# A lightning-attention and routed-experts block on one core: base projection behind the transposes, routing inside the rounds, experts' second product inside the attention phase

## The chip, the core and the metric

The kernel runs on one core of a Trainium2 chip. A core has five engines with an instruction queue each, and every queue is worked off in order: TensorE (PE, matrix products and transposes), VectorE (DVE), ScalarE (ACT), GpSimd (POOL) and SyncE (SP), which here issues all DMAs. The metric is the device time of one execution in microseconds, as a median over several; beside it stands a profile of a single execution. All data are fp32. A matrix product of fp32 shows in the records as two passes of PE.

## The reference

With x of 2 x 512 tokens and width 512, and xn = layernorm(x):

```python
x = x + _L0_attn_ref(xn, ...) + _L0_ffn_ref(xn, ...)

# attention: 32 heads of 128, linear attention with decay, blocks of 32
qkv = silu(xn @ qkv_w.T)                 # q, k, v
scores = q k^T * diag_decay ; intra = scores v ; inter = (q * q_decay) kv
attn = intra + inter, normalised over all heads (rms), times norm_w
out = (sigmoid(xn @ gate_w.T) * normed) @ out_w.T

# experts: 8 low-rank experts of rank 16, the two largest logits per token
logits = x_flat @ W_router.T ; combine = weights of the top 2, else 0
h = einsum('nd,erd->ner', x_flat, A) ; hw = h * combine[:, :, None]
expert_out = einsum('ner,eor->no', hw, B) * 2
base_out = x_flat @ W_base.T + b_base
```

The feed-forward half (base_out + expert_out) depends only on xn and meets the attention half in the last addition.

## The kernel before

Tokens are eight tiles of 128 (t = 0 to 7). The kernel has four stages.

**Setup** (lines 204 to 335, pool `sp`). SP loads the eight tiles `x`, the router and A weights `wra`, the base weights `wbase`, `bias`, `wlb` (B), and the first two weight sets `raw`. For each tile, DVE normalises (L242 to L248), PE transposes it into a bank `fr` (L252), ACT copies it to `xnT` (L253), PE makes logits and h at once in bank `ra` (L257, recorded under the helper `mm`, L80), and ACT copies them to `lg` and `hl` (L259, L260). `base(t)` (L227) makes the base product in one of four banks `seeded` (in the profile `sd`); it is called three tiles behind the transposes, and DVE adds it to x (L233). Then come the routing on DVE (L278 to L300: two maxima over the logits, their weights, `hl` multiplied by them), sums of `xnT` (`xsum`, L306 to L309, and `xt`, L316 to L319), the bias additions on POOL (L321), and the experts: transposes of `hl` (L326), a copy to `hT` (L329), the product with `wlb` (L333), an addition on DVE (L334) and a store to `x_kept` in DRAM (L335).

**Rounds** (lines 354 to 470, pools `aw` and `aw2`). v and gate of all heads are made with a two-level Strassen scheme: 56 rounds of 7 inner products. `encode` (L173) makes the weight sums on POOL two rounds ahead (`s`, five buffers, and `e`, three); `inner_product` (L354) is PE's; `after` (L386) takes results out of the banks on ACT and DVE into `sum`, `y`, `w`, `c` and `z` (six buffers), and `result` (L374) applies Silu or Tanh and stores v and gate to DRAM. The first two rounds read only the first batch's xnT. `SLOTS` (L443) gives the order by hand: a round's last two products run in the next round.

**Attention** (lines 473 to 690, pool `work`). Loop over i = 0 to 65, two for each head (L652). In each iteration a new `attend` begins (L543), two older ones go on, and parts of the next heads' q and k projections (`unit`, L491) are put between. v and gate come back from DRAM two iterations ahead (`load_vg`, L533, five buffers each). `attend` ends with the output in a bank `at` (two of them), its square on ACT (`sq`, two buffers, L585), the sum of squares on POOL (L586), the gated product on DVE (L588) and a store (L589).

**Output projection** (from L690). It loads `x_kept` back as a whole (`x_back`, L743) and adds it at the end (`finish`, L709).

What sets the order: the code's order gives each instruction its priority; the framework that builds the program orders every engine's queue beforehand, with a model of the times, and takes a later instruction where nothing earlier is ready. So the first sums of the attention's weights (L126) stand on POOL at 49 us, although `load_unit` is called near the end of the rounds. On the chip that order is fixed. Memory of a closed pool is given to the next one, and a tile there waits for the old tiles' last readers.

Of the kernel before, what the change touches and what calls it, by code (L numbers as in the profile page):

```python
# [59 lines left out]
def attn_moe_kernel(ctx: ExitStack, tc: tile.TileContext, x, qk_w, v_w, gate_w, out_w, norm_w,  # L60
# [15 lines left out]
    def bank(tag):  # L76
        return ps.tile([P, 512], F32, tag=tag, name=f"ps_{tag}", bufs=banks[tag])

    def mm(o, lhsT, rhs, start, stop):
        nc.tensor.matmul(o, lhsT, rhs, start=start, stop=stop)  # L80
# [3 lines left out]
    ident = keep.tile([P, P], F32, tag="ident", name="ident")  # L84
    ones = keep.tile([P, 1], F32, tag="ones", name="ones")
    nw = keep.tile([P, H], F32, tag="nw", name="nw")
    xnT = [wts.tile([P, KC, S], F32, tag=f"xnT{b}", name=f"xnT{b}") for b in range(B)]
# [5 lines left out]
                          for i in range(NG // 2)] for n in ("v", "gate"))  # L93
    x_kept = dram.tile([P, NT, HID], F32, tag="x_kept", name="x_kept")

# [77 lines left out]
    def encode(n, q):  # L173

        def outer(k, a, b, op):
            t = sums2[n, k] = aw.tile([P, 2, 2, 256], F32, tag="s", name="s", bufs=5)
            nc.gpsimd.tensor_tensor(t, a, b, op)
# [24 lines left out]


    xt = [aw.tile([P, 4, S // 2], F32, tag=f"xt{q}", name=f"xt{q}") for q in range(1, 8)]
    with tc.tile_pool(name="setup", bufs=1) as sp:
# [4 lines left out]
        wbase = sp.tile([P, KC, HID], F32, tag="wbase", name="wbase")  # L210
        wlb = sp.tile([P, HID], F32, tag="wlb", name="wlb")
        bias = sp.tile([P, HID], F32, tag="bias", name="bias")
        for t in range(NT):
# [3 lines left out]
        nc.sync.dma_start(wbase, base_w)  # L217
        nc.sync.dma_start(bias, base_b.partition_broadcast(P))
        nc.sync.dma_start(wlb, lora_b)
        load_set(0)  # L220
# [6 lines left out]
        def base(t):  # L227

            b, tt = divmod(t, TB)
            bp = seeded[t % 4]  # L230
            for c in range(KC):
                mm(bp, xnT[b][:, c, tt * P : (tt + 1) * P], wbase[:, c, :], c == 0, c == KC - 1)
            nc.vector.tensor_tensor(x_sb[t], x_sb[t], bp, ALU.add)  # L233


        lg = sp.tile([P, NT, NE], F32, tag="lg", name="lg")
        hl = sp.tile([P, NT, NE, R], F32, tag="hl", name="hl")
        stats = sp.tile([P, NT, 6], F32, tag="stats", name="stats")
        mv = sp.tile([P, NT, 2], F32, tag="mv", name="mv")
        for g, ts in enumerate(((0,), (1, 2), (3, 4, 5), (6, 7))):  # L240
# [4 lines left out]
            for i, t in enumerate(ts):  # L245
# [14 lines left out]
                nc.scalar.copy(hl[:, t].rearrange("p e r -> p (e r)"), ra[:, NE : NE + ER])  # L260
                if t > 2:
                    base(t - 3)
        for t in range(NT - 3, NT):
            base(t)

        prio = sp.tile([P, NT, NE], F32, tag="prio", name="prio")
        for e in range(NE):
            nc.gpsimd.memset(prio[:, :, e : e + 1], float(NE - e))

        def small(name, shape):  # L270
            return sp.tile(shape, F32, tag=name, name=name)

        def wide(v):
            return v.unsqueeze(2).to_broadcast([P, NT, NE])

        def largest(lg_, n):
            m, c, hit = small(f"m{n}", [P, NT]), small(f"c{n}", [P, NT]), small(f"hit{n}", [P, NT, NE])
            nc.vector.tensor_reduce(m, lg_, AX.X, ALU.max)  # L278
            nc.vector.tensor_tensor(hit, lg_, wide(m), ALU.is_equal)
            nc.vector.tensor_tensor(hit, hit, prio, ALU.mult)  # L280
            nc.vector.tensor_reduce(c, hit, AX.X, ALU.max)
            nc.vector.tensor_tensor(hit, hit, wide(c), ALU.is_equal)
            return m, hit

        m1, hit1 = largest(lg, 1)
        lg2 = small("lg2", [P, NT, NE])
        nc.vector.scalar_tensor_tensor(lg2, hit1, LOWEST, lg, ALU.mult, ALU.add)
        m2, hit2 = largest(lg2, 2)

        e2, w1, w2 = (small(n, [P, NT]) for n in ("e2", "w1", "w2"))  # L290
        nc.vector.tensor_tensor(e2, m2, m1, ALU.subtract)
        nc.scalar.activation(e2, e2, AF.Exp)
        nc.vector.tensor_scalar_add(w1, e2, 1.0)
        nc.vector.reciprocal(w1, w1)
        nc.vector.tensor_scalar_mul(w1, w1, SCALING)
        nc.vector.tensor_tensor(w2, w1, e2, ALU.mult)
        nc.vector.tensor_tensor(hit1, hit1, wide(w1), ALU.mult)
        nc.vector.tensor_tensor(hit2, hit2, wide(w2), ALU.mult)
        nc.vector.tensor_tensor(hit1, hit1, hit2, ALU.add)
        nc.vector.tensor_tensor(hl.rearrange("p t e r -> p (t e) r"),  # L300
                                hl.rearrange("p t e r -> p (t e) r"),
                                hit1.rearrange("p t e -> p (t e)").unsqueeze(2).to_broadcast([P, NT * NE, R]),
                                ALU.mult)

# [15 lines left out]
        for t in range(NT):  # L320
            nc.gpsimd.tensor_tensor(x_sb[t], x_sb[t], bias, ALU.add)  # L321

        for q in range(NT // 4):
            tp = bank("fr")
            for i in range(4):
                nc.tensor.transpose(tp[:, i * P : (i + 1) * P],  # L326
                                    hl[:, q * 4 + i].rearrange("p e r -> p (e r)"), ident)
            hT = sp.tile([P, 4 * P], F32, tag="hT", name="hT", bufs=2)
            nc.scalar.copy(hT, tp)  # L329
            for i in range(4):  # L330
                t = q * 4 + i
                lp = seeded[i]
                mm(lp, hT[:, i * P : (i + 1) * P], wlb, True, True)  # L333
                nc.vector.tensor_tensor(x_sb[t], x_sb[t], lp, ALU.add)  # L334
                nc.sync.dma_start(x_kept[:, t, :], x_sb[t])  # L335

# [49 lines left out]
    def after(r, i):  # L386
# [6 lines left out]
        def out_of(ij, v, more=None, c=None):  # L393

            for src, to in adds:
                if isinstance(to, str):
                    o = outer_sums[n, to][:, ij]
                else:
                    o = temp("z", 6)
                if more is not None and (src is None or one):  # L400
# [39 lines left out]
        elif i == 4:  # L440
            out_of(2, st["pd"])

    SLOTS = ((0, 1), (0, 5), (0, 2), (1, 7), (0, 6), (0, 3), (1, 4))  # L443
    for k in range(7 * len(rounds) + 7):
        r0, m = divmod(k, 7)
        if m == 0:
            if r0 + 2 < len(rounds):
                encode(*rounds[r0 + 2])
# [94 lines left out]
    def attend(head, b):  # L543
# [37 lines left out]
        if head == 0:  # L581
            nc.scalar.activation(ssq[b], pa, AF.Square)
        else:
            sq = tmp("sq", 2)
            nc.scalar.activation(sq, pa, AF.Square)  # L585
            nc.gpsimd.tensor_tensor(ssq[b], ssq[b], sq, ALU.add)  # L586
# [15 lines left out]
    for _ in projections(0):  # L602
        pass

    HT, HO = S // 2, HID // 2
# [46 lines left out]
    for i in range(H * B + 2):  # L652
        p, part = divmod(i, 4)
        if part == 0:
# [7 lines left out]
            if p == NP - 1:  # L662
# [4 lines left out]
                for j in range(EARLY):  # L667
                    operands(0, j)
        load_vg(i + 2)
        if i < H * B:  # L670
            running[i] = attend(*divmod(i, B))
# [143 lines left out]
```

## Time and profile before

| | us |
|---|---|
| median of 3 runs | 1240.96 (1240.21 to 1243.94) |
| the profiled execution | 1241.71 |
| its span, first to last instruction | 1239.9 |
| setup, to the first round's steady work | 0 to 76.5 |
| rounds | 76.5 to 433 |
| attention | 433 to about 1051 |
| output projection, to the end | about 1051 to 1239.9 |

The page gives, for each engine, busy time and its share of the span, then the span in 40 slices of 31 us. Groups of instructions are named by line, engine, operation and tiles (written <- read), with count, busy time and mean ns of one, and the idle time of the engine before them with what ended it. Busy time of PE is modelled at the ends of its passes, so the distance from start to start is the better measure of what one pass costs. The granted clock tells which share of full speed PE was allowed in a stretch.

### The profile page before, as it was taken

The page shows a single profiled execution, that of the slowest core. Times are in us where ns is not written, and L with a number is a line of the kernel's source. Part 1 is how long each engine was busy: PE and PEld are TensorE (multiplying, and loading weights), DVE is VectorE, ACT ScalarE, POOL GpSimd, SP SyncE. Part 2 cuts the span into 40 slices and gives each one's busy share as a digit, 9 for nine tenths or more (in the row PEclk, how much of TensorE's full clock was granted, in tenths as well). Part 3 has the DMA queues.
Part 4 walks back from the last instruction along what each step waited for, and adds up shares of the span by engine and source line. Part 5 has one row for each costly group of instructions (what it writes and reads, how often), then busy time and mean ns, then how long its engine had stood idle before and what let it go on. Part 6 is the DMA issues. An engine that isn't in the chain of part 4 may idle for free.

```text
span 1239.9 us, 17100 instructions
## 1 busy us (share of the span) xinstructions
PE 1207.4 (97%) x6328; PEld 914.3 (74%) x6328; DVE 629.1 (51%) x1104; ACT 366.1 (30%) x648; POOL 592.8 (48%) x662
## 2 busy tenths in 40 slices
PE   6789999999999999999999999999999999999998
PEld 4369889899899745666666666666666669888887
DVE  5757666766766624444444434444444444455333
ACT  2124444444444422223222222222232332320000
POOL 3926568758756241434433433433333343655552
PEclk9989999999999999999999999999999999999999
DMA  8012543452442353343443443343334333843221
GB/s 315 0 68 75 173 151 121 153 170 96 161 161 103 123 166 91 119 135 112 145 140 103 125 134 102 117 125 118 116 114 128 120 97 108 309 150 122 93 92 52
DMA packets 102706, 158.17 MB, mean 128 GB/s; under 512 B 8800, under 2 KB 68192, under 8 KB 101344
## 3 DMA queue, kind: packets, MB, share of 16 engines
q1 hardware_dynamic: 102624, 157.09, 38.2%
q8 instruction: 50, 0.82, 0.3%
q14 instruction: 32, 0.26, 0.1%
HBM read 102.53 MB, written 54.53 MB: 127 GB/s over the span
## 4 chain that ended last, share of the span: by engine, by line
PE 93%; DVE 5%; issue 1%; ACT 1%; DMA 0%; SPq 0%; DVEq 0%; ACTq 0%
PE ps_ch L488 31%; PE ps_ch L645 9%; PE ps_at L80 8%; PE ps_sc L80 8%; PE ps_fr L362 7%; PE ps_fr L366 7%; PE sd L362 5%; PE sd L366 5%; PE ps_sc L645 4%; PE ps_at L645 2%; PE sd L80 2%; PE ps_sc L550 2%; DVE z L405 1%; DVE sum L405 1%; PE ps_ra L80 1%
## 5 line engine op out<-in xcount | busy, mean ns | idle before, releaser
L488 PE MATMUL ps_ch<-xsum,ws 128*128 128x512 f32 x384 | 180.0, 593 | 0.0
L562 POOL TENSOR_TENSOR qd<-q,mask 128x384 f32<-128x384 f32 x64 | 64.2, 1003 | 219.9 <-PE ps_at L80 214.8
L488 PE MATMUL ps_ch<-xnT,w 128*128 128x512 f32 x256 | 122.2, 600 | 0.8 <-DVE z L405 0.8
L488 PEld LDWEIGHTS ps_ch<-xsum,ws 128*128 128x128 f32 x384 | 68.5, 191 | 63.2 <-issue 63.2
L80 PEld LDWEIGHTS ps_at<-scores,v 128*128 128x128 f32 x512 | 77.4, 192 | 28.0 <-issue 27.7
L126 POOL TENSOR_TENSOR ws<-w 128x256 f32<-128x256 f32 x32 | 23.4, 730 | 154.3 <-DMA w<-in_qk_w 154.3
L503 DVE TENSOR_TENSOR c<-ps_ch,u 128x512 f32<-128x512 f32 x96 | 66.4, 691 | 58.4 <-PE ps_ch L488 58.4
L588 DVE SCALAR_TENSOR_TENSOR gT<-gate,ps_at 128x512 f32<-128x512 f32 x64 | 44.0, 687 | 97.5 <-ACT sq L585 94.5
L645 PE MATMUL ps_ch<-wsum,gsum 128*128 128x256 f32 x384 | 89.1, 379 | 0.0
L80 PE MATMUL ps_at<-scores,v 128*128 128x128 f32 x512 | 88.4, 275 | 0.0
L585 ACT ACTIVATE sq<-ps_at 128x512 f32<-128x512 f32 x62 | 37.0, 597 | 155.2 <-PE ps_at L80 155.1
L586 POOL TENSOR_TENSOR ssq<-ssq,sq 128x512 f32<-128x512 f32 x62 | 79.2, 1278 | 6.5 <-ACT sq L585 6.5
L645 PEld LDWEIGHTS ps_ch<-wsum,gsum 128*128 128x128 f32 x384 | 72.3, 190 | 9.5
L80 PE MATMUL ps_at<-qd,state 128*128 128x128 f32 x384 | 74.2, 275 | 0.0
L80 PEld LDWEIGHTS ps_sc<-v,kd 128*128 128x128 f32 x384 | 52.8, 191 | 28.4 <-issue 28.2
L633 POOL TENSOR_TENSOR wsum<-wo 128x256 f32<-128x256 f32 x32 | 25.3, 790 | 93.0 <-PE ps_ch L645 37.4
L488 PEld LDWEIGHTS ps_ch<-xnT,w 128*128 128x128 f32 x256 | 44.4, 192 | 34.2 <-issue 33.1
L503 DVE TENSOR_TENSOR u<-ps_ch,p 128x512 f32<-128x512 f32 x32 | 22.1, 692 | 91.4 <-PE ps_ch L488 85.5
L80 PE MATMUL ps_sc<-q,k 128*128 128x128 f32 x512 | 67.6, 275 | 0.0
L552 ACT ACTIVATE kd<-ps_sc,mask 128x384 f32<-128x384 f32 x64 | 37.2, 580 | 89.8 <-PE ps_sc L550 89.8
L626 DVE TENSOR_TENSOR gsum<-gated 128x256 f32<-128x256 f32 x32 | 15.1, 470 | 95.2 <-PE ps_sc L645 66.7
L80 PEld LDWEIGHTS ps_sc<-q,k 128*128 128x128 f32 x512 | 62.2, 192 | 0.0
(224 smaller groups left out, 2633.6 us busy)
## 6 DMA issues: line engine op xcount, KB each, us to landing
w<-in_qk_w SPq DMA_DIRECT2D x32, 512.0 KB, 4.1
v_kept<-z SPq DMA_DIRECT2D x64, 256.0 KB, 2.4
gate_kept<-z SPq DMA_DIRECT2D x64, 256.0 KB, 2.4
v<-v_kept SPq DMA_DIRECT2D x64, 256.0 KB, 2.6
gate<-gate_kept SPq DMA_DIRECT2D x64, 256.0 KB, 3.2
g_kept<-gT SPq DMA_DIRECT2D x64, 256.0 KB, 2.5
gated<-g_kept SPq DMA_DIRECT2D x32, 512.0 KB, 3.7
raw<-in_v_w SPq DMA_DIRECT2D x8, 1024.0 KB, 6.6
```

What stands on the lines that cost most here:

```text
L80: nc.tensor.matmul(o, lhsT, rhs, start=start, stop=stop)
L362: nc.tensor.matmul(o[:, (2 * u + j) * P : (2 * u + j + 1) * P], x_[:, j * P : (j + 1) * P], a[:, u], start=first and u == 0 and j == 0, st ...
L366: nc.tensor.matmul(o[:, u * HB : (u + 1) * HB], a[:, u], x_, start=first and u == 0, stop=True, skip_group_check=True)
L488: nc.tensor.matmul(o, a[:, c, :], b[:, c, :], start=first and c == 0, stop=c == 1, skip_group_check=True)
L503: nc.vector.tensor_tensor(o, p, t, ALU.add)
L552: nc.scalar.activation(kd.rearrange("p j d -> p (j d)"), pk[:, : (TB - 1) * P], AF.Copy, scale=mask[:, 0, P - 1 : P])
L562: nc.gpsimd.tensor_tensor(qd, q[:, P:].rearrange("p (j n) -> p j n", j=TB - 1), mask[:, 1, :].unsqueeze(1).to_broadcast([P, TB - 1, P]), A ...
L585: nc.scalar.activation(sq, pa, AF.Square)
L586: nc.gpsimd.tensor_tensor(ssq[b], ssq[b], sq, ALU.add)
L588: nc.vector.scalar_tensor_tensor(gT, gate.pop((head, b)), 1.0, pa, ALU.add, ALU.mult)
L633: nc.gpsimd.tensor_tensor(t[:, 0], b12, b11, ALU.subtract)
L645: nc.tensor.matmul(sums[n][:, i * HO : (i + 1) * HO], l[:, i * P : (i + 1) * P], r, start=p == 0 and i == 0, stop=p == NP - 1, skip_group_ ...
```

## The change

The base product of all eight tiles is called after the transposes, the routing products and the sums `xt`; ACT copies it out and SP stores it to a new DRAM tensor `x_base`, without bias, x or experts. Routing is a function `route()`, called at the beginning of the third round (r0 == 2); it replaces exp and reciprocal by a tanh of half the difference of the two logits. `transpose_experts()` is called at the beginning of the sixth round (r0 == 5) and leaves `hT` in memory that lives to the end. The second product is a function `experts(t)`, called in the attention loop at i = 8, 12, ... 36: two loads, two additions on POOL, the product into a bank `at`, an addition on DVE, a store. `lg` and `hl` move to `aw`; `s`, `z` and `sq` have one buffer less. `bias` and `wlb` are loaded at the start of the attention phase.

```diff
-            t = sums2[n, k] = aw.tile([P, 2, 2, 256], F32, tag="s", name="s", bufs=5)
+            t = sums2[n, k] = aw.tile([P, 2, 2, 256], F32, tag="s", name="s", bufs=4)
...
-        nc.sync.dma_start(bias, base_b.partition_broadcast(P))
-        nc.sync.dma_start(wlb, lora_b)
...
             for c in range(KC):
                 mm(bp, xnT[b][:, c, tt * P : (tt + 1) * P], wbase[:, c, :], c == 0, c == KC - 1)
-            nc.vector.tensor_tensor(x_sb[t], x_sb[t], bp, ALU.add)
+            o = sp.tile([P, HID], F32, tag="based", name="based", bufs=3)
+            nc.scalar.copy(o, bp)
+            nc.sync.dma_start(x_base[:, t, :], o)
...
-                if t > 2:
-                    base(t - 3)
-        for t in range(NT - 3, NT):
-            base(t)
...
         for t in range(NT):
-            nc.gpsimd.tensor_tensor(x_sb[t], x_sb[t], bias, ALU.add)
-        for q in range(NT // 4):
...
+            base(t)
...
-                    o = temp("z", 6)
+                    o = temp("z", 5)
...
+    def transpose_experts():
+        for q in range(2):
+            tp = bank("ra")
+            for i in range(4):
+                nc.tensor.transpose(tp[:, i * P : (i + 1) * P],
+                                    hl[:, q * 4 + i].rearrange("p e r -> p (e r)"), ident)
+            nc.scalar.copy(hT[:, 4 * q : 4 * q + 4, :], tp.rearrange("p (t n) -> p t n", t=4))
+
+    def route():
+        prio = aw.tile([P, NT, NE], F32, tag="prio", name="prio")
+        for e in range(NE):
+            nc.gpsimd.memset(prio[:, :, e : e + 1], float(NE - e))
...
+        def largest(lg_, n):
+            m = temp("w")[:, :NT] if n == 1 else small(f"m{n}", [P, NT])
+            c, hit = small(f"c{n}", [P, NT]), small(f"hit{n}", [P, NT, NE])
+            nc.vector.tensor_reduce(m, lg_, AX.X, ALU.max)
+            nc.vector.tensor_tensor(hit, lg_, wide(m), ALU.is_equal)
+            nc.vector.tensor_tensor(hit, hit, prio, ALU.mult)
+            nc.vector.tensor_reduce(c, hit, AX.X, ALU.max)
+            nc.vector.tensor_tensor(hit, hit, wide(c), ALU.is_equal)
+            return m, hit
+
+        m1, hit1 = largest(lg, 1)
+        nc.vector.scalar_tensor_tensor(lg, hit1, LOWEST, lg, ALU.mult, ALU.add)
+        m2, hit2 = largest(lg, 2)
+        w1, w2 = (small(n, [P, NT]) for n in ("w1", "w2"))
+        nc.vector.tensor_tensor(w2, m1, m2, ALU.subtract)
+        nc.scalar.activation(w2, w2, AF.Tanh, scale=0.5)
+        nc.vector.tensor_scalar(w1, w2, SCALING / 2, SCALING / 2, ALU.mult, ALU.add)
+        nc.vector.tensor_scalar(w2, w2, -SCALING / 2, SCALING / 2, ALU.mult, ALU.add)
+        nc.vector.tensor_tensor(hit1, hit1, wide(w1), ALU.mult)
+        nc.vector.tensor_tensor(hit2, hit2, wide(w2), ALU.mult)
+        nc.vector.tensor_tensor(hit1, hit1, hit2, ALU.add)
+        nc.vector.tensor_tensor(hl.rearrange("p t e r -> p (t e) r"),
+                                hl.rearrange("p t e r -> p (t e) r"),
+                                hit1.rearrange("p t e -> p (t e)").unsqueeze(2).to_broadcast([P, NT * NE, R]),
+                                ALU.mult)
...
         if m == 0:
+            if r0 == 2:
+                route()
+            if r0 == 5:
+                transpose_experts()
...
-            sq = tmp("sq", 2)
+            sq = tmp("sq", 1)
...
+    wlb = work.tile([P, HID], F32, tag="wlb", name="wlb")
+    bias = work.tile([P, HID], F32, tag="bias", name="bias")
+    nc.sync.dma_start(wlb, lora_b)
+    nc.sync.dma_start(bias, base_b.partition_broadcast(P))
+
+    def experts(t):
+        o, x_ = tmp("rest", 2), tmp("rest", 2)
+        nc.sync.dma_start(o, x_base[:, t, :])
+        nc.sync.dma_start(x_, x[t * P : (t + 1) * P, :])
+        nc.gpsimd.tensor_tensor(o, o, bias, ALU.add)
+        nc.gpsimd.tensor_tensor(o, o, x_, ALU.add)
+        lp = bank("at")
+        mm(lp, hT[:, t, :], wlb, True, True)
+        nc.vector.tensor_tensor(o, o, lp, ALU.add)
+        nc.sync.dma_start(x_kept[:, t, :], o)
...
         load_vg(i + 2)
+        if i >= 8 and i % 4 == 0 and i // 4 - 2 < NT:
+            experts(i // 4 - 2)
```

More of the change, by code (lines that the diff above doesn't have):

```diff
@@ L85, in attn_moe_kernel @@
     ones = keep.tile([P, 1], F32, tag="ones", name="ones")
+    hT = keep.tile([P, NT, P], F32, tag="hT", name="hT")
     nw = keep.tile([P, H], F32, tag="nw", name="nw")
@@ L93, in attn_moe_kernel @@
                           for i in range(NG // 2)] for n in ("v", "gate"))
-    x_kept = dram.tile([P, NT, HID], F32, tag="x_kept", name="x_kept")
+    x_kept, x_base = (dram.tile([P, NT, HID], F32, tag=n, name=n) for n in ("x_kept", "x_base"))
     def inv_sqrt(sp, mean_sq, n, name, scale=None):
@@ L201, in attn_moe_kernel @@
     rounds.append((NSET - 1, 4))
+    lg = aw.tile([P, NT, NE], F32, tag="lg", name="lg")
+    hl = aw.tile([P, NT, NE, R], F32, tag="hl", name="hl")
     xt = [aw.tile([P, 4, S // 2], F32, tag=f"xt{q}", name=f"xt{q}") for q in range(1, 8)]
@@ L210, in attn_moe_kernel @@
         wbase = sp.tile([P, KC, HID], F32, tag="wbase", name="wbase")
-        wlb = sp.tile([P, HID], F32, tag="wlb", name="wlb")
-        bias = sp.tile([P, HID], F32, tag="bias", name="bias")
         for t in range(NT):
@@ L232, in base @@
                 mm(bp, xnT[b][:, c, tt * P : (tt + 1) * P], wbase[:, c, :], c == 0, c == KC - 1)
-            nc.vector.tensor_tensor(x_sb[t], x_sb[t], bp, ALU.add)
-        lg = sp.tile([P, NT, NE], F32, tag="lg", name="lg")
-        hl = sp.tile([P, NT, NE, R], F32, tag="hl", name="hl")
+            o = sp.tile([P, HID], F32, tag="based", name="based", bufs=3)
+            nc.scalar.copy(o, bp)
+            nc.sync.dma_start(x_base[:, t, :], o)
         stats = sp.tile([P, NT, 6], F32, tag="stats", name="stats")
@@ L260, in attn_moe_kernel @@
                 nc.scalar.copy(hl[:, t].rearrange("p e r -> p (e r)"), ra[:, NE : NE + ER])
-                if t > 2:
-                    base(t - 3)
-        for t in range(NT - 3, NT):
-            base(t)
[L266 to L303, printed above, removed]
         b11, b12, b21, b22 = xnT[0][:, 0:2], xnT[1][:, 0:2], xnT[0][:, 2:4], xnT[1][:, 2:4]
@@ L320, in attn_moe_kernel @@
         for t in range(NT):
-            nc.gpsimd.tensor_tensor(x_sb[t], x_sb[t], bias, ALU.add)
-        for q in range(NT // 4):
[L324 to L335, printed above, removed]
+            base(t)
     aw2 = phase_a.enter_context(tc.tile_pool(name="aw2", bufs=1))
@@ L441, in after, with small, wide @@
             out_of(2, st["pd"])
+    def transpose_experts():
[9 more added lines that the diff above has]
+            nc.gpsimd.memset(prio[:, :, e : e + 1], float(NE - e))
+        def small(name, shape):
+            return aw.tile(shape, F32, tag=name, name=name)
+        def wide(v):
+            return v.unsqueeze(2).to_broadcast([P, NT, NE])
+        def largest(lg_, n):
[22 more added lines that the diff above has]
+                                ALU.mult)
     SLOTS = ((0, 1), (0, 5), (0, 2), (1, 7), (0, 6), (0, 3), (1, 4))
```

## The prediction

> **What bounds the kernel now.** I read the page first: the engines' shares, then the slices. Columns of the first line are busy microseconds and share of the span.
>
> ```profile
> PE 1207.4 (97%) x6328; PEld 914.3 (74%) x6328; DVE 629.1 (51%) x1104; ACT 366.1 (30%) x648; POOL 592.8 (48%) x662
> ...
> PE   6789999999999999999999999999999999999998
> ...
> PEclk9989999999999999999999999999999999999999
> ```
>
> PE is the bound: whatever it neither waits for nor executes comes off the span almost one for one. Its 32.5 us without work (1239.9 - 1207.4) lie mostly in the first slices, where PEclk also dips: 11.0 pass before the first operand. The stretches of 10 us there (busy time and count of PE, PEld, DVE, ACT, POOL, then granted clock):
>
> ```profile
> 40.00:50.00 10.00, 10.00 (x26) 4.50 (x25) 10.00 (x11) 1.62 (x3) 10.00 (x7) 1.00 0.00 0
> 50.00:60.00 10.00, 3.03 (x8) 1.01 (x6) 10.00 (x15) 0.21 (x1) 9.84 (x11) 0.90 0.00 1
> 60.00:70.00 10.00, 4.49 (x13) 3.20 (x14) 9.01 (x25) 1.17 (x2) 4.45 (x3) 0.50 0.00 0
> 70.00:80.00 10.00, 10.00 (x45) 6.26 (x44) 5.23 (x8) 0.57 (x1) 0.00 (x0) 0.92 0.55 211
> ```
>
> From 53 us PE stands still while DVE and POOL are full, and when PE resumes it has half its clock. The list of waits names the cause, the timeline (start, duration) the order:
>
> ```profile
> PE ps_fr L326 <- DVE hl L300: 12.5, 1, 12.5
> ```
>
> ```profile
> 39.99 13.04 PE L80 MATMUL sd<-wbase,xnT 128*128 128x512 f32 x30
> ...
> 64.24 1.21 DVE L300 TENSOR_TENSOR hl<-hl,hit 128x1024 f32<-128x1024 f32 x1
> ...
> 65.51 1.97 PE L326 MATMUL ps_fr<-ident,hl 128*128 128x128 f32 x8 [12.48 <-DVE hl L300]
> ...
> 67.27 0.64 PE L362 MATMUL ps_fr<-raw,xnT 128*128 128x128 f32 x2
> ...
> 67.70 8.97 PE L80 MATMUL sd<-wlb,hT 128*128 128x512 f32 x16
> ...
> 76.50 0.83 PE L362 MATMUL ps_fr<-raw,xnT 128*128 128x128 f32 x6
> ```
>
> So: base projection ends at 53.03; the experts' transposes wait for the routing's last DVE operation; after them come the experts' products, and only then, at 76.50, the rounds go on. None of that is needed by the rounds.
>
> **Part 1, the stretch that goes.** 53.03 to 76.50 is 23.47 us. Two passes of the first round were done inside it and must still be done: 2 x 0.11 (passes of this kind follow each other every 0.11 us after 76.50). Gone from the setup: **23.25 us**.
>
> **Part 2, where the rounds can start instead.** Their PE predecessor is the base product. From 17.64 to 53.03 PE had no gap: pairs of base passes stand between the router products of two tiles (router products begin at 18.61 and 20.40, a base pair at 19.54). Moving base(t) behind the transposes lowers its priority but not PE's sum, so with such filling it again ends at 53. Were nothing filled in, router products 1.8 us apart would end at about 20.4 + 4 x 1.8 + 1.1 = 28.7, with 6 x 0.95 + 4 x 0.45 = 7.5 us of work in 11.1: 3.6 lost. The seen filling is nearer: **0.3**. First operands: set 0's e is ready at 25.97. DVE loses the eight base additions (5.5 us), the eight of the experts' results (5.5) and the routing from this stretch; its xsum and xt take 25.9 us in all, of which 21 after the last transpose (38.9 at the latest), so they end by 60 at worst, and the third round, the first to need them, starts at 53 + 12.3. Covered, by 5 us. ACT gets eight base copies of 0.58 where it is 16% busy. The bias and wlb loads leave the start, so the weight sets land earlier, which nobody waits for before 53, and queue behind the first v loads of the attention phase, 70 us ahead of their use.
>
> The rounds' temporaries lie in memory that the setup gives up, the last piece of it after base(7)'s copy (0.58 on ACT, the row of the xnT copy) and its DMA (2.0 to landing, the x_kept row, plus about 0.5 to issue): near 56.5, while y of the first round is wanted near 55. Bounds 0 and 3 us; most of that memory is free long before: **0.5**.
>
> **Part 3, routing in the rounds.** The old 20 DVE operations took 9.74 us (summed from their rows); four small ones of 0.16 to 0.19 become two, so 9.4. In the first four rounds, of 6.15 us each from 76.50, DVE is busy 0.94, 1.93, 3.46 and 4.05 us: 14.2 us free. It fits if it starts in the first, and in rounds 2 to 5 (2.7 + 2.1 + 2.2 + 2.6 = 9.6 free) only just. Queued behind each operation on DVE are evictions of the PSUM banks, for which PE waits. Here **a rule speaks against the change**: the Trainium skill, "SBUF — State Buffer", Who interferes with whom, says that a DVE instruction with two SBUF inputs and a GpSimd one that reads SBUF lock each other out for a whole instruction. The rows agree: the hit operation of L282 took 0.75 once and 1.27 once, z<-c averages 1.31 us against 0.69 for one with a PSUM input. By the rule, each of the twelve two-input routing operations could wait out a POOL addition of 0.75 us: 9.4 could become up to 18 and overrun the 9.6 by some 8. But 9.4 was itself measured with POOL at 98 to 100%, and POOL is at 0 to 46% in the first three rounds, so I keep the row. PE stall: between 0 and 8, I take **1.5**. Exp's own table load (1.28 on ACT) becomes the Tanh load, which the rounds' L379 needed anyway. The single hold of a w buffer by m1 leaves one, enough while w is read before the next is written.
>
> The transposes move to the sixth round: 8 x 0.11, **1.0** with seams, at full clock. They share one bank, so the second four wait for an ACT copy of 0.58: between 0 (round products in between) and 0.8, **0.4**. s loses one of five buffers, z one of six: the second set's second s then waits for the fifth round's last product, 6 us ahead of its use, and takes 2.4; z(k) would start at the nearest 1.7 us after z(k-5) has landed (starts and landings of all 128 z; 2.5 us after the issue where no landing is recorded). Both nothing; without that cover each late z costs what it is late.
>
> **Part 4, experts in the attention phase.** Rows that price it:
>
> ```profile
> L80 PE MATMUL sd<-wlb,hT 128*128 128x512 f32 x16 | 9.0, 724 | 0.0
> L586 POOL TENSOR_TENSOR ssq<-ssq,sq 128x512 f32<-128x512 f32 x62 | 79.2, 1278 | 6.5 <-ACT sq L585 6.5
> L588 DVE SCALAR_TENSOR_TENSOR gT<-gate,ps_at 128x512 f32<-128x512 f32 x64 | 44.0, 687 | 97.5 <-ACT sq L585 94.5
> ```
>
> and, from SP's list of waits:
>
> ```profile
> SPq L541 <- PE ps_at L80: 316.0, 59, 8.2
> ```
>
> PE: 16 passes of 0.43 (their spacing after 71.8) = **6.9**, exposed, since PE is at 100% here. POOL: 16 additions x 1.28 = 20.5 us in some 260 us where POOL works 40%; DVE: 8 x 0.69. SP issues three more DMAs per call (x_base, x, x_kept), beside eight x_base stores in setup, behind which only masks and w of the attention phase are queued. SP waits 316 us in the v loads anyway, because it runs ahead, so three issues of 0.5 fit; behind them stand v and gate loads with five buffers. POOL in order could hold up qd and ssq behind an addition waiting for its load; ssq is followed by the square of the next call, which now shares the only sq buffer. Through iteration 36 that square starts at least 5 us after the previous addition's end; less than 4 is seen only after 1034 us (down to -0.4, with ACT at a third). Nothing in the likely case. If the cover is gone: rival B.
>
> **The clock.** From 65.51 to about 71.5 every pass took double. The Trainium skill, "TensorE: Matmul & The Clock Gate", What's actually happening, says that the gate opens after one busy window of about 3.4 us; by that rule the moved work would get 1.7 us cheaper, by the rows 3.0 (6.0/2). Part 1 uses the rows; by the rule the total would be 1.3 us less gain.
>
> **Sum.** -23.25 + 0.3 + 0.5 + 1.5 + 1.0 + 0.4 + 6.9 = -12.65. The profiled execution's span 1239.9 becomes 1227.2 (its time 1241.71 becomes 1229.1); the median 1240.96 becomes **1228.3 us**.
>
> **The rivals.**
> A, DVE becomes the bound in the rounds: routing late, PE waits at the hl transposes as it did before, and drops to half clock. For it: exactly this wait was 12.5 us, with DVE at 100%. Against it: five rounds (31 us) now lie between. Taking 8 us for the overrun in place of 1.5, plus 2 of half clock: 1228.3 + 8.5 = 1236.8.
> B, slower: the additions on POOL wait for the x_base and x loads, sq's single buffer passes the wait to ACT and PE. Place: the eight calls. It eats the gain from 12.65/8 = 1.6 us each, and is slower than 0.3% from 2.0 each. POOL did wait 4 to 6 us per weight unit for its w load; 2.5 us of that reaching PE eight times, 20 us, gives 1248. Against it: those waits cost PE nothing so far.
> C, none of the small stalls appears, nor the clock dip between rounds and attention (granted 0.91 from 420 to 440, worth 1.8): 1228.3 - 2.7 - 1.8 = 1224.
> That the planner puts base early after all changes nothing: PE's sum is the same.
>
> **How the numbers follow.** Likeliest case 0.62, its own range 1224.5 to 1233 (stalls of 0 to 6); A 0.17 (1233 to 1240); B 0.09; C 0.12. 0.3% is 3.7 us, about what this measurement tells from no change: 1237.2 to 1244.7. Faster: 0.62 + 0.12 + 0.10 of A = 0.84; same: 0.07 of A and a little of B, 0.08; slower 0.08. Range 1222 to 1238: it leaves out B, the far end of A and the edge of C.
>
> **What would show it.** No wait of PE for hl; PE gapless around 53, with round products right behind base; no granted clock of 0.5 in the setup after 20 us; about 23 us between the old and new start of the rounds, 2 to 5 of it given back by their end, and 7 by iteration 40. The forecast is wrong if PE waits for hl or DVE in the rounds, or if the distance shrinks by over 1.6 us at each expert call.

## The result and the profile after

The changed kernel takes **1226.66 us** as a median of four runs (1225.80 to 1227.79). The kernel before, run beside it, took 1240.59 (1240.16 to 1243.94). The ratio is 0.9885, with a 95% interval of 0.987 to 0.990: 1.15% faster. The prediction was 1228.3, with a range of 1222 to 1238. The profiled execution of the changed kernel took 1225.9 us, its span is 1224.1, so in the profiles the distance is 15.8 us.

The page of the changed kernel, first the shares of the engines and then the slices, shows PE's first slices filled and its clock no longer marked down:

```profile
PE 1204.5 (98%) x6328; PEld 912.2 (75%) x6328; DVE 629.2 (51%) x1094; ACT 370.2 (30%) x656; POOL 599.0 (49%) x670
...
PE   6999999999999999999999999999999999999998
...
PEclk9999999999999999999999999999999999999999
```

PE's busy time fell by 2.9 us only; the rest of the 15.8 was standstill. The stretches of 10 us (columns as before: length, busy time and count of PE, PEld, DVE, ACT, POOL, then granted clock, DMA share, GB/s) show where:

```profile
40.00:50.00 10.00, 10.00 (x25) 4.50 (x24) 10.00 (x14) 1.49 (x3) 8.84 (x11) 1.00 0.21 79
50.00:60.00 10.00, 10.00 (x60) 7.90 (x59) 2.06 (x5) 4.66 (x9) 0.00 (x0) 1.00 0.14 52
60.00:70.00 10.00, 9.56 (x71) 9.01 (x71) 8.42 (x23) 4.88 (x8) 5.39 (x8) 1.00 0.01 2
```

In 50 to 60 PE is full, where it had 3.03 busy before, and the clock stays at 1.00. PE's timeline (start, duration) has no gap behind the base product:

```profile
39.57 13.47 PE L80 MATMUL sd<-wbase,xnT 128*128 128x512 f32 x31
52.87 1.05 PE L304 MATMUL ps_fr<-raw,xnT 128*128 128x128 f32 x8
53.77 1.06 PE L304 MATMUL ps_fr<-e,xt 128*128 128x128 f32 x8
...
69.50 1.13 PE L308 MATMUL sd<-xt,raw 128*128 128x256 f32 x4 [0.44 <-DVE sum L343]
...
83.08 0.60 PE L390 MATMUL ps_ra<-ident,hl 128*128 128x128 f32 x4
83.52 1.06 PE L304 MATMUL ps_fr<-s,xsum 128*128 128x128 f32 x8
84.41 0.60 PE L390 MATMUL ps_ra<-ident,hl 128*128 128x128 f32 x4
```

The base product ends at 53.04, as before (53.03), and the rounds follow at once. The only visible trace of the routing is the gap of 0.44 us at 69.50 (with the passes about it, 0.7 us from start to start). The experts' transposes stand in two groups of four with a product of the rounds between them, so the single bank costs nothing. In the list of waits nothing is left of the wait for `hl`; PE's largest waits are the start and two at the end of the rounds:

```profile
PE ps_fr L251 <- DVE ln1y L111: 11.1, 1, 11.1
PE sd L308 <- DVE z L343: 1.2, 1, 1.2
PE ps_ch L483 <- DVE z L347: 0.8, 1, 0.8
```

**Where the time went.** Take the same instruction of both kernels at several places and subtract the starts. In the rounds that is the copy of `sd` that ACT makes once per round, in the attention phase the square of each `attend`:

| place | distance, us | step |
|---|---|---|
| rounds 1 to 3 | 23.4 to 23.6 | the stretch is gone |
| round 4 | 22.8 | -0.7, routing |
| round 6 | 21.8 | -1.0, transposes |
| last round | 20.9 | -0.9, the sum of steps from -1.1 to +1.8 |
| first square of attention | 22.6 | +1.7, clock |
| iterations 8 to 36 | 22.6 to 15.8 | 8 x -0.86, products |
| end | 15.8 | 0.06 |

### The profile page after: what moved, and what is told of

Same layout as the page of the kernel before. It is cut to its first block, busy times and chain, and to the rows that moved or that the text cites. A ratio compares the mean times of both kernels' runs of the same rounds, so it can differ in the third digit from the quotient of the medians.

```text
span 1224.1 us, 17092 instructions
## 1 busy us (share of the span) xinstructions
PE 1204.5 (98%) x6328; PEld 912.2 (75%) x6328; DVE 629.2 (51%) x1094; ACT 370.2 (30%) x656; POOL 599.0 (49%) x670
## 4 chain that ended last, share of the span: by engine, by line
PE 91%; DVE 6%; ACT 1%; issue 1%; DMA 0%; SPq 0%; DVEq 0%; ACTq 0%
PE ps_ch L483 31%; PE ps_ch L657 9%; PE ps_at L80 9%; PE ps_sc L80 8%; PE ps_fr L308 7%; PE ps_fr L304 6%; PE sd L308 5%; PE ps_sc L657 5%; PE sd L304 4%; PE ps_at L657 2%; PE sd L80 2%; DVE sum L347 2%; DVE z L347 2%; PE ps_sc L545 2%; PE ps_ra L80 1%
## 5 line engine op out<-in xcount | busy, mean ns | idle before, releaser
L127 POOL TENSOR_TENSOR ws<-w 128x256 f32<-128x256 f32 x32 | 23.6, 738 | 158.6 <-DMA w<-in_qk_w 158.6
L554 DVE TENSOR_TENSOR scores<-ps_sc,mask 128x512 f32<-128x512 f32 x64 | 44.2, 691 | 33.4 <-PE ps_sc L80 33.4
```

The costliest lines, as they stand in the source:

```text
L554: nc.vector.tensor_tensor(sc, pc.rearrange("p (j n) -> p j n", j=TB), mask[:, 0, :].unsqueeze(1).to_broadcast([P, TB, P]), ALU.mult)
```

## The experiments

Each kernel ran on one chip with the kernel before beside it, and its ratio is to those runs. Differences of two changed kernels are read from the traces where they are under 0.3%.

Two theories stood at the start. T1: routing's place between the base product and the rounds made the long wait, and where base stands is of no matter. T2: base had to move behind the transposes so that VectorE could begin earlier.

### Base back between the transposes

```diff
                 nc.scalar.copy(hl[:, t].rearrange("p e r -> p (e r)"), ra[:, NE : NE + ER])
+                if t > 2:
+                    base(t - 3)
+        for t in range(NT - 3, NT):
+            base(t)
...
-        for t in range(NT):
-            base(t)
```

> The changed kernel with the base product called between the transposes again, three tiles behind, as before; all else stays changed. Theory T1 (the gain is the wait for hl, which went because routing, transposes and products left the setup; PE's sum in the setup is the same in either order): 1226.7 within 1, base ends near 53. Theory T2 (base behind the transposes is what pays, because DVE's sums of xnT start 11 us earlier): without it xsum starts at 38.9 again and the xt end near 60; the third round needs them at 65, so T2 expects 1226.7 to 1230, more than 1 above the changed kernel.

Measured: 1226.54 us (1225.02 to 1226.88), ratio 0.9888 [0.9871, 0.9906], the same as the changed kernel. PE's timeline again joins base and rounds without a gap:

```profile
44.55 8.32 PE L80 MATMUL sd<-wbase,xnT 128*128 128x512 f32 x19
52.70 1.05 PE L306 MATMUL ps_fr<-raw,xnT 128*128 128x128 f32 x8
```

The sums `xt` ended at 53.4 instead of 51.4, still before the third round needs them. With routing in the rounds, the place of base is worth nothing; T2 fell here.

### Routing back in the setup, then the transposes too

Routing goes back behind the router products in the setup (base stays behind the transposes, the experts' transposes in the sixth round); in the second kernel the transposes also go back ahead of the first round. The function moves as a whole, and `m1` then has a buffer of its own. The comments in this cut and the next are this document's.

```diff
+        route()                       # setup, ahead of xsum and xt; its definition moves with it
...
-            if r0 == 2:
-                route()
             if r0 == 5:               # second kernel: r0 == 0
                 transpose_experts()
```

> The changed kernel with the routing back in the setup, ahead of the sums of xnT, its transposes still in the sixth round. If routing on DVE costs PE 1.5 us in the rounds, as the prediction has it, this gains 0.7 to 1.5: 1225.2 to 1226. If instead DVE is now too late with xt for the third round (about 8 us of routing ahead of the last xt, which end at 51.4 in the changed kernel, so 59 to 61 against a need at 65): no loss either. A rival that DVE in the setup is the bound after all: 1228 or more.

> As the run with routing in the setup, but with the eight transposes of hl and their two copies ahead of the first round instead of in the sixth; PE's and ACT's queues differ in nothing else, DVE's not at all. T1 taken strictly (routing in the setup brings the wait back): PE stands 4 to 10 us before the transposes and falls to half clock for some us, 1231 to 1238. T2: routing starts 11 us earlier than in the kernel before (xsum at 27.2 instead of 38.9), hl is done about 26.5 - 3.4 us after that (the distance in the kernel before without its base additions), at 50 to 53: no wait or under 1.5, 1226 to 1228.

Measured: 1232.06 us (1231.32 to 1233.01), ratio 0.9932 [0.9917, 0.9948], and 1232.66 us (1231.15 to 1232.86), ratio 0.9934 [0.9918, 0.995]. Both expectations missed. The first kernel was to be as fast as the changed one and lost 5.4 us; the second has no wait for `hl`, which is ready at 52.0, as T2 had it; its time lies in the range that T1 gave for that wait, but not by it. The loss of both is a wait that neither theory had. The list of PE's waits of the first, and ACT's timeline:

```profile
PE sd L80 <- ACT based L233: 4.6, 1, 4.6
```

```profile
28.80 0.59 ACT L233 COPY based<-sd 128x512 f32<-128x512 f32 x1 [1.38 <-PE sd L80]
29.40 1.28 ACT L290 ACT_TABLE_LOAD   x1
46.39 0.21 ACT L290 ACTIVATE w<-w 128x8 f32<-128x8 f32 x1 [15.71 <-DVE w L289]
46.51 1.54 ACT L233 COPY based<-sd 128x512 f32<-128x512 f32 x3
```

Routing's tanh stands second on ACT's queue among the base copies. It waits 15.7 us for VectorE, the copies behind it wait with it, no base bank is emptied, and PE stops for 4.6 us within the base product and then has half a clock for some 6 us (0.82 and 0.84 as means of 40 to 50 and 50 to 60). The base product ends at 60.7 and the rounds begin 7.7 us later than in the changed kernel; they get 0.7 back where routing is missing from them. So routing in the rounds has a second use: with ScalarE taking base out, an ACT instruction of the routing must not stand ahead of base's copies.

### Base between the transposes and routing in the setup

This is the order of the kernel before in all but the base copies on ACT, the bias, the late products, routing's tanh and the buffers.

```diff
 # as the second kernel above, and
+                if t > 2:
+                    base(t - 3)       # between the transposes
+        for t in range(NT - 3, NT):
+            base(t)
...
-        for t in range(NT):
-            base(t)                   # behind them
```

> Base between the transposes, routing in the setup and the transposes of hl ahead of the first round; only the experts' products, the output of base by ACT and the buffers stay changed. Both theories expect the wait for hl back: xsum starts at 38.9, hl is done near 62, PE stands 8 to 10 us and then runs at half clock for about 6 (3 lost): 1237 to 1240. If it stays below 1230, the wait came from DVE's base additions and from nothing else.

Measured: 1227.47 us (1226.62 to 1229.25), ratio 0.9897 [0.988, 0.9914]. A miss of both theories: with routing and transposes where they had been, nearly the whole gain remains. VectorE finishes `hl` at 53.8 instead of 65.5, and PE waits 2.1 us instead of 12.5. **T1 fell too**: routing's place alone did not make the long wait. What differs from the kernel before on the way to `hl` is VectorE's own base additions, GpSimd's additions of bias, a fifth `s`, and routing's tanh. Two new theories follow, D (VectorE had too much to do) and L (GpSimd locked it out). The next two kernels put parts back one at a time; a third starts from the kernel before and takes the buffers away.

### Base added by VectorE again

```diff
-            o = sp.tile([P, HID], F32, tag="based", name="based", bufs=3)
-            nc.scalar.copy(o, bp)
-            nc.sync.dma_start(x_base[:, t, :], o)
+            nc.vector.tensor_tensor(x_sb[t], x_sb[t], bp, ALU.add)
...
+        for t in range(NT):           # after xt; experts() no longer loads or adds x
+            nc.sync.dma_start(x_base[:, t, :], x_sb[t])
```

> As the kernel with base between the transposes, routing in the setup and the transposes ahead of the first round (1227.5 us, routing's result ready at 53.8 us), but VectorE adds base into x as it did before, in place of ScalarE's copies; the sum is stored once and the expert calls load that alone. Theory D (VectorE's own additions queued the routing late): four additions of 0.69 us fall between the first xsum and the routing's result, and their loads on PSUM delay others; the result is ready at 57 or later and the median is 1230 to 1233. Theory L (the long wait was made by GpSimd's additions locking VectorE out): the result comes only the four additions later, at about 56.4, PE waits some 4.5 us instead of 2.1, and the median is 1229 to 1230.

Measured: 1231.09 us (1227.99 to 1232.45), ratio 0.9924 [0.9904, 0.9943]. `hl` is ready at 54.95, only 1.2 us later, and PE waits 2.9 us, below what either theory said. The median nevertheless lies in D's interval, and the traces do not show why: behind the wait both kernels have half a clock for 3.4 us (from 54.7 us there, from 56.5 here), and the two profiled executions are 0.8 us apart. The intervals of the two ratios overlap. By the place where the result becomes ready, D is too large.

### GpSimd's bias additions back in the setup

```diff
         for t in range(NT):
+            nc.gpsimd.tensor_tensor(x_sb[t], x_sb[t], bias, ALU.add)
             nc.sync.dma_start(x_base[:, t, :], x_sb[t])
...
-        nc.gpsimd.tensor_tensor(o, o, bias, ALU.add)      # in experts()
```

> As the previous kernel, with GpSimd's eight additions of bias back in the setup and bias loaded there. Theory L: VectorE's routing and xt operations stretch from 0.21 and 0.41 us to 0.74 and about 1 us wherever a GpSimd addition runs, the routing's result comes another 5 to 9 us later (61 to 65), PE's wait for it is 9 to 12.5 us as it was before the change, and the median is 1234 to 1238. Theory D: nothing is added to VectorE's queue, so the result moves by less than 1.5 us and the median by less than 2.

Measured: 1237.90 us (1236.40 to 1241.30), ratio 0.9984 [0.9976, 0.9991]. Nearly the whole gain is gone. The lists of PE's waits of the three kernels, in the order ACT copies, VectorE's additions, GpSimd's additions as well:

```profile
PE ps_ra L434 <- DVE hl L300: 2.1, 1, 2.1
```

```profile
PE ps_ra L434 <- DVE hl L298: 2.9, 1, 2.9
```

```profile
PE ps_ra L437 <- DVE hl L300: 10.1, 1, 10.1
```

Putting eight additions back on GpSimd makes 7.2 us of PE's wait, although VectorE's queue has not one instruction more: from the first `xsum` to `hl` it works on 36 operations in both, in 16.8 us and in 24.0. The groups of VectorE in 36 to 68 us (busy time, mean ns of one), without GpSimd's additions and then with them, show what lengthened:

```profile
L232 DVE TENSOR_TENSOR x<-x,sd 128x512 f32<-128x512 f32 x5 | 3.4, 678 | 4.2 <-PE sd L80 4.2
...
L306 DVE TENSOR_TENSOR xsum<-xnT,xnT 128x1024 f32<-128x1024 f32 x1 | 1.2, 1226 | 0.4 <-ACT xnT L250 0.4
L298 DVE TENSOR_TENSOR hl<-hl,hit 128x1024 f32<-128x1024 f32 x1 | 1.2, 1215 | 0.0
...
L281 DVE TENSOR_TENSOR hit<-hit,prio 128x64 f32<-128x64 f32 x2 | 0.4, 214 | 0.0
```

```profile
L308 DVE TENSOR_TENSOR xsum<-xnT,xnT 128x1024 f32<-128x1024 f32 x1 | 4.6, 4597 | 0.4 <-ACT xnT L252 0.4
L234 DVE TENSOR_TENSOR x<-x,sd 128x512 f32<-128x512 f32 x5 | 3.4, 678 | 4.2 <-PE sd L80 4.2
...
L300 DVE TENSOR_TENSOR hl<-hl,hit 128x1024 f32<-128x1024 f32 x1 | 2.3, 2282 | 0.0
...
L283 DVE TENSOR_TENSOR hit<-hit,prio 128x64 f32<-128x64 f32 x2 | 1.5, 744 | 0.0
```

The same operation takes 1.23 or 4.60 us. Operations with an input in PSUM do not show it: the base additions (`x<-x,sd`) take 678 ns in both kernels. The Trainium skill, "SBUF — State Buffer", Who interferes with whom, says that a VectorE instruction with two SBUF inputs contends with a GpSimd one that reads SBUF, and that one with at most one SBUF input does not; these rows agree with both halves.

Not all of the 7.2 us stands beside the additions themselves, as GpSimd's timeline of the second kernel shows:

```profile
36.90 1.31 POOL L323 TENSOR_TENSOR x<-x,bias 128x512 f32<-128x512 f32 x1
38.13 0.77 POOL L193 TENSOR_TENSOR e<-e,s 128x256 f32<-128x256 f32 x1
...
40.18 1.31 POOL L323 TENSOR_TENSOR x<-x,bias 128x512 f32<-128x512 f32 x1
...
52.34 3.95 POOL L323 TENSOR_TENSOR x<-x,bias 128x512 f32<-128x512 f32 x3
```

Three small operations of VectorE at 52.4 to 56.4 us and `hl` itself, all beside additions, grow by 4.2 us together. The first `xsum` (37.97 us) grows by 3.4, but beside two additions and three sums of `e`, which the additions pushed back; without the additions these sums had ended at 37.3, before `xsum` began at 38.2. Theory L holds: 7.2 us is what the eight additions of 1.3 cost together with the order that they bring on GpSimd.

### The three buffer cuts alone

```diff
-            ... tag="s", name="s", bufs=5)
+            ... tag="s", name="s", bufs=4)
-                    o = temp("z", 6)
+                    o = temp("z", 5)
-            sq = tmp("sq", 2)
+            sq = tmp("sq", 1)
```

> The kernel before with the three buffer cuts of the change alone: s four instead of five, z five instead of six, sq one instead of two. The prediction costed all three at nothing: the median stays within 0.3% of the kernel before, 1240.6 plus or minus 1.5. If z's margin of 1.7 us is too thin or the square waits for GpSimd, PE waits appear on z or sq and the time grows by 2 us or more. One thing could make it faster: with four s buffers GpSimd's fifth s cannot be made ahead in the setup.

Measured: 1236.81 us (1235.59 to 1238.41), ratio 0.9966 [0.995, 0.9982]: the cuts make the kernel before **faster**. The timelines, before and then with the cuts, at the fourth `xsum`, with GpSimd's fifth `s` beside it before, and, with the cuts, at PE's wait:

```profile
44.25 2.34 POOL L177 TENSOR_TENSOR s<-raw 128x1024 f32<-128x1024 f32 x1
44.29 3.38 DVE L309 TENSOR_TENSOR xsum<-xnT,xsum 128x1024 f32<-128x1024 f32 x1
```

```profile
43.73 1.21 DVE L309 TENSOR_TENSOR xsum<-xnT,xsum 128x1024 f32<-128x1024 f32 x1
...
62.79 1.97 PE L326 MATMUL ps_fr<-ident,hl 128*128 128x128 f32 x8 [10.30 <-DVE hl L300]
```

In the kernel before, GpSimd made a fifth `s` (2.34 us) at 44.25, and the `xsum` beside it took 2.2 us longer. With four buffers that addition can't be made so early, and PE's wait falls from 12.5 to 10.3. In the rounds the cuts work both ways: a wait of 1.82 us for ACT at 160.43 shrinks to 0.34, and steps elsewhere cost more than that, so that the rounds as a whole give 1.3 us back; which of the cuts does this was not separated. Of the 4.3 us between the spans of the two profiles, 1.7 is the clock dip at 433 us of the kernel before, which is missing from the execution with the cuts; that the cuts removed it isn't shown.

With this the whole wait is taken apart, in one order of steps. Others may share out the interactions differently; routing in the rounds with the bias additions left in the setup was not run.

| step | PE's wait for hl | ratio to before |
|---|---|---|
| kernel before | 12.5 | 1 |
| buffers cut | 10.3 | 0.9966 [0.995, 0.9982] |
| products late, tanh | 10.1 | 0.9984 [0.9976, 0.9991] |
| bias on GpSimd later | 2.9 | 0.9924 [0.9904, 0.9943] |
| base out by ACT | 2.1 | 0.9897 [0.988, 0.9914] |
| base behind, routing and transposes in the rounds | none | 0.9885 [0.987, 0.99] |

### Without the routing

```diff
-            if r0 == 2:
-                route()
```

> The changed kernel without the routing (the two largest logits are not sought and their weights not applied; the experts' transposes and products remain). The prediction's step of 1.5 us for routing in the rounds says 1225.2; the trace of the changed kernel says that round 3 alone lost 0.7 us, so 1226.0. Rival A, with VectorE the bound in the rounds, says 1220 or less. In the trace the rounds should reach their end 0.7 us (1.5 by the prediction) earlier after a start at the same place.

Measured: 1225.83 us (1224.86 to 1227.26), ratio 0.9886 [0.9869, 0.9903]. This execution came into the rounds 0.63 us later than the changed kernel and left round 4 0.07 earlier, so routing in the rounds costs 0.7 us; the spans differ by 0.1, because of the later start, whose cause is open.

### Without the products, and with two sq buffers

```diff
-        lp = bank("at")
-        mm(lp, hT[:, t, :], wlb, True, True)
-        nc.vector.tensor_tensor(o, o, lp, ALU.add)
```

> The changed kernel without the experts' second product and VectorE's addition of it (the eight calls still load base and x and add the bias). The prediction's step of 16 passes of 0.43 us, exposed on PE, says 6.9 us less: 1219.8. If a part of the products hid in PE's waits it is 3 to 6; if the calls cost more than their passes (rival B) the eight calls give back over 8 us. In the trace the distance to the changed kernel should grow by 0.86 us per call and nowhere else.

Measured: 1226.39 us (1225.58 to 1227.22), ratio 0.9889 [0.9875, 0.9904]: nothing was gained. Over the eight calls the distance grows by 0.86 us each and 6.87 in all, as the prediction's price says. But ahead of that 7.2 us are lost in one place, by PE's wait for `state` and the half clock behind it:

```profile
PE ps_sc L80 <- DVE state L567: 3.9, 1, 3.9
```

Taking the products out changed the order of the rest. In the changed kernel the eight loads of `x_base` are spread from 426.7 to 712.9 us, since each call holds its buffers until its product; without it all eight fall in 424.8 to 479.9, and their additions bunch on GpSimd. There the square waited 3.8 us for an addition of `ssq` that stood behind them, through the single `sq` buffer. The last run gives `sq` its second buffer back:

```diff
-            sq = tmp("sq", 1)
+            sq = tmp("sq", 2)
```

> The kernel without the experts' products (and without the now unused load of wlb), with two sq buffers instead of one. Without products the eight calls' additions bunch on GpSimd in 424 to 489 us; with one sq, ScalarE's square waited 3.8 us at 490.9 for the addition of ssq behind them, g_kept's store, the next gated load and VectorE's state came late, and PE waited 3.9 us at 503.6 and then ran at half clock: 6.3 us in all, which ate the 6.9 of the products. If the single sq is the link, two of them let the square go on time, no PE wait of over 1.5 us is left near 500, and the median is 1219.5 to 1221.5. If the bunched additions delay qd or the weights' sums by themselves, PE still waits over 3 us there and the median stays above 1224.

Measured: 1231.03 us (1229.46 to 1231.74), ratio 0.9928 [0.9906, 0.995], and PE's wait is 7.7 us: worse. The square is on time now, but PE is late by another way. The timeline:

```profile
490.86 1.27 POOL L608 TENSOR_TENSOR rest<-rest 128x512 f32<-128x512 f32 x1 [0.16 <-DMA rest<-in_x]
492.16 0.33 SPq L609 DMA_DIRECT2D x_kept<-rest  x1
...
493.05 0.52 SPq L584 DMA_DIRECT2D g_kept<-gT  x1
...
497.46 0.52 SPq L584 DMA_DIRECT2D g_kept<-gT  x1
...
502.29 0.32 SPq L627 DMA_DIRECT2D gated<-g_kept  x1
...
506.74 0.65 DVE L633 TENSOR_TENSOR gsum<-gated 128x256 f32<-128x256 f32 x1 [11.43 <-DMA gated<-g_kept]
...
507.64 2.08 PE L80 MATMUL ps_sc<-q,k 128*128 128x128 f32 x8 [7.65 <-DVE state L567]
```

The store of `x_kept` waits on SP for GpSimd's addition, and the stores of `gT` queue behind it: the `gT` made at 488.28 is stored at 497.46, where in the changed kernel the store follows within a microsecond (`gT` at 488.6, store at 489.3). The kernel with one `sq` had this delay too (`gT` at 479.31, store at 489.63). Then the load of `gated`, VectorE's `gsum` in front of `state`, and PE follow in a row. So the single `sq` is not the only link, and the expectation that it is fell. What both kernels share is the bunch of eight calls in 60 us; whether spreading them would by itself remove the stall was not tried.

### Four more GpSimd additions in each call

```diff
+        for _ in range(2):
+            nc.gpsimd.tensor_tensor(o, o, bias, ALU.add)
+            nc.gpsimd.tensor_tensor(o, o, bias, ALU.subtract)
```

> The changed kernel with four more GpSimd additions of the bias in each of the eight expert calls (twice added, twice taken off): 4 x 1.28 = 5.1 us of GpSimd per call, 41 in all. Theory: loads and additions are issued a whole call ahead and GpSimd is 40% busy, so the median moves by less than 1 us. Rival B (the single sq buffer passes GpSimd's delay to ScalarE and PE): from 4.5 us of delay a call, the least margin seen there, the square waits, and the eight calls give back 0.6 us or more each, 1231.5 or above.

Measured: 1226.00 us (1225.16 to 1227.63), ratio 0.9878 [0.9859, 0.9898]. The distance of its squares to those of the changed kernel is 0.57 us at the first and at the last. With calls spread as they are, 5 us more of GpSimd in each cost nothing: rival B's cover is real there.

### Transposes in the gap at the end of the rounds

```diff
-            if r0 == 5:
-                transpose_experts()
+        if r0 == len(rounds) and m == 6:
+            transpose_experts()
```

> The changed kernel with the eight experts' transposes moved from the sixth round into the seven steps after the last round, where PE stands 1.2 us for VectorE. If the prediction's step of 1.0 us for the transposes is PE work on the path and the gap takes it up, the median is about 1.0 lower, 1225.7, and the rounds end 1.0 us earlier. If the gap is set by something the transposes delay (the copy of ScalarE, the one bank), it is the same, 1226.7.

Measured: 1225.21 us (1224.86 to 1226.60), ratio 0.9873 [0.9854, 0.9891]. The sixth round gets 0.96 us back. At the end PE's timeline shows the gap filled, with a wait of its own for the single bank's copy:

```profile
407.93 0.60 PE L390 MATMUL ps_ra<-ident,hl 128*128 128x128 f32 x4
409.27 0.66 PE L390 MATMUL ps_ra<-ident,hl 128*128 128x128 f32 x4 [0.74 <-ACT hT L392]
409.76 1.03 PE L308 MATMUL sd<-xt,raw 128*128 128x256 f32 x4
```

In the traces 0.67 us remain of it. That is the least time of all kernels here, but its interval overlaps that of the changed kernel, so it isn't shown to be better.

## Why the prediction was right, and where not

**Part 1, the stretch that goes (23.25), and part 2 (0.3 and 0.5).** Right in size: 23.4 measured against 22.45 in sum, since neither small loss came. The base product ended at 53.04 behind the transposes, and at 52.87 between them; "lowers its priority but not PE's sum" holds. No round's temporary waited for memory: PE has no gap near 55 to 57. The sums `xt` ended at 51.4, 14 us ahead of their need.

The mechanism held: what stood between the base product and the rounds left PE's path, whatever had made it long. The reading of why it was long was wrong. "The list of waits names the cause" took the end of the routing as a thing of its place. The list named the last link; the runs show that VectorE was late mostly because GpSimd's additions locked it out (of the 12.5 us, 7.2 with the additions of bias and 2.2 with a fifth `s`), and little for its own base additions (0.8). The prediction weighed the lock only for the new place of the routing, and there kept the row; it did not ask what the lock did in the old place, where its own rows (0.75 and 1.27 for the same `hit`) showed it.

**Part 3, routing 1.5.** 0.7 measured, by the trace of the changed kernel and by the run without it. GpSimd is busy 5.4 of the 10 us from 60 to 70, and the 18 routing operations took 7.2 us against 9.7 for the 20 before. So "9.4" was too high (its rows held the lock of the old place), and the 18 of the rule never near. VectorE's timeline at the end of the routing:

```profile
67.40 0.77 DVE L426 TENSOR_TENSOR hit<-hit,w 128x64 f32<-128x64 f32 x1
68.09 0.76 DVE L427 TENSOR_TENSOR hit<-hit,w 128x64 f32<-128x64 f32 x1
68.77 0.68 DVE L343 TENSOR_TENSOR sum<-sd,y 128x512 f32<-128x512 f32 x1
```

Two operations, lengthened from 0.21 us beside GpSimd's sums of `e` (67.36 to 69.4), stand ahead of the eviction for which PE waited 0.44 us: that is the mechanism of rival A, at a twentieth of its size.

The **transposes (1.0)** cost 0.97. **The single bank (0.4)** cost nothing, as products stood between; in the last gap, where none did, it cost 0.74. That Exp's table load "becomes the Tanh load, which the rounds' L379 needed anyway" was wrong: ACT loads a table for routing's tanh at 65.22 and another for the rounds at 72.15, 1.28 us each. Neither delayed PE.

**The cuts of s and z, "both nothing".** Wrong: alone they move the time by -0.34%. The margins were read for lateness only. That a later start takes work out of a crowded stretch was missed. In the changed kernel, where the stretch is gone, only what they do in the rounds is left: the long wait at 160 us shrinks by 1.8 here too, steps elsewhere cost more, and 0.9 us is lost in sum, with the same signs at the same rounds as in the kernel with the cuts alone.

**Part 4, products 6.9.** 6.87 measured in eight steps of 0.86. The additions, loads and stores were hidden, as said, and stay hidden with 5 us more of GpSimd. Rival B did not come in this kernel. In the two kernels without products, where the calls lay bunched, GpSimd's additions did reach PE: 7 and 11 us were lost, in one place and not in each call.

**The clock.** Part 1 counted 3.0 us of gain from the half clock behind the wait, by the row (6.1 us of it in the trace), against an estimate of 1.7 by the page "TensorE: Matmul & The Clock Gate", What's actually happening. It went altogether with the wait, and is within the 23.4. Rival C's 1.8 between rounds and attention was also gained in the profile (granted clock 1.00 from 410 to 440, after the same gaps of 1.23 and 0.78 us as before); the executions of the changed kernel lie in two pairs, near 1225.9 us with a granted clock of 1.000 and near 1227.6 with 0.998, about one such dip apart.

**The sum.** -12.65 predicted. In the profiles: -23.4 - 0.1 (drift over the first rounds) + 0.7 + 1.0 + 0.9 - 1.7 + 6.9 - 0.1 = -15.8. In the medians it is -13.9: two of the four executions of the changed kernel seem to have such a dip, and the profiled one of the kernel before was 1.1 above its median. The mechanism was right; of the terms, routing (0.8 too much), memory, filling and bank (1.2 too much) and the clock were mis-sized, and the unseen 0.9 of the buffers went the other way.

## What to carry to other kernels

A long wait names its last link, not its cause: compare the durations of the same operation inside and outside the crowded stretch, and look at who else was working. In the order of steps tried here, moving eight GpSimd additions out of VectorE's critical stretch was worth more (0.6% in the ratios) than moving base, routing and transposes after that (0.1%, not clear of noise). When an operation goes to another engine, look up what stands ahead of it in that engine's queue and in SP's: one instruction that waits there stops all behind it. And an experiment that takes work away also changes the order of what remains, so read its steps in the trace, not its total.

## What the runs showed of the hardware

- Two-input VectorE operations beside GpSimd: a 128x1024 sum took 1.21 to 1.23 us alone and 3.38 or 4.60 beside GpSimd, a 128x64 one 0.21 and 0.74. With one PSUM input the 128x512 addition took 678 ns in both kernels. GpSimd's own 128x256 sums took 0.73 to 0.74 us otherwise and 1.7 beside VectorE's sums (39 to 48 us of the kernel before).
- The half clock after a standstill lasted about 6.1 us (kernel before, wait of 12.5), 3.4 (cuts alone, wait of 10.3) and 6.1 (without products, wait of 3.9). So both the row that the prediction used and the rule that it set against it are met, and the length does not follow the wait's.
- With the standstill's own part, the granted clock was 0.5 for 13.65 us in the kernel before (57.93 to 71.59), 10.24 with the cuts alone (55.96 to 66.20), 6.83 without products (502.84 to 509.67) and 3.41 in the dip at 433.40: four, three, two and one times 3.41. In the first three it ended with the first of these steps of 3.41 us in which PE worked throughout, which began 2.7, 0.0 and 2.7 us after PE had resumed; this agrees with the 6.1, 3.4 and 6.1 behind the waits.
- After waits of 2.1 us (base by ACT) and 2.9 us (base added by VectorE again) the first passes ran at full speed; the half clock came 0.8 and 1.4 us after PE had resumed, at 54.7 and 56.5, and lasted 3.4 us.
